# The reciprocal standard deviation of a layer norm, moved from ScalarE's square root to Newton steps on VectorE

## The chip, the cores and the metric

The kernel runs on one core of a Trainium2 chip. A core has five engines with an instruction stream each: TensorE (PE in the profile, its weight loads PEld), VectorE (DVE), ScalarE (ACT), GpSimd (POOL) and SyncE (SP, which here only issues transfers). They run beside each other and wait for each other's results through semaphores. The metric is the time of one execution on the device in microseconds (us); smaller is better.

## The reference

A graph network of two layers with residuals on 32768 nodes of 256 features, and 524288 edges sorted by target. Layer 0 is attention inside 256 blocks of 128 nodes; layer 1 sends messages along the edges in both directions and updates each node through a gate. Each layer begins with a layer norm over a node's 256 features, and relu:

```python
def _layernorm(x, axis=-1, eps=1e-5):
    m = jnp.mean(x, axis=axis, keepdims=True)
    v = jnp.var(x, axis=axis, keepdims=True)
    return (x - m) / jnp.sqrt(v + eps)

h = jnp.maximum(_layernorm(x, axis=-1), 0.0)
x = x + layer0(h, ...)        # out = softmax(Q K^T * scale + bias) V, then Wo
h = jnp.maximum(_layernorm(x, axis=-1), 0.0)
x = x + layer1(h, src, dst, edge_weight, edge_weight_n2, ...)

# layer 1: batch norm over the nodes, then
a_in  = segment_sum(feat_in[src]  * iw[:, None], dst)
a_out = segment_sum(feat_out[dst] * ow[:, None], src)
# xi = [a_in, a_out] @ W_x2i + b; gates: sigmoid, tanh; h = new + gate * (h - new)
```

What the change touches is the factor 1/sqrt(v + eps) of both layer norms: one number for each node.

## The kernel before, in words

Four parts follow each other. Up to about 960 us the edges are sorted into items, tables are made and the attention bias is gathered. Then comes the **merged stage** (1159 to 10272 us), which does two things beside each other: all of layer 0 (layer norm, attention, the second layer norm), and, edge by edge, the copying of layer-1 rows into source order. A gather stage up to 17.6 ms and a last stage of gates and output follow. The change lies in the merged stage and in the two groups of nodes that are worked off alone ahead of it (964 to 1158 us).

**The edge loop.** The edges are cut into items of 128. A round is 64 items, and each item is one step, about 2 us long. There are 68 rounds, in three phases; most are unrolled by four, and a phase's last rounds run singly. In a step (`items`, lines 1139 to 1145) the engines do, in an order written out by hand:

- `fetch` (line 1089): SP loads 128 rows of the normalised h1, 12 steps ahead;
- `spread_lanes` (1095), every fourth step: four small matmuls, 4 steps ahead;
- `select` (1099, 1100): DVE makes a one-hot matrix `oh`, 2 steps ahead, and every fourth step the selection `selT`;
- `rank` (1111): three matmuls of PE add the one-hot matrices into the running counts `R`;
- `product` (1106): PE picks each edge's row of h1;
- `place` (1123): DVE reads from `R` the place of each edge; every fourth step (1127) it adds the four together into `pi`;
- `scale` (1115, 1117): ACT multiplies the picked rows by the edge's weight, one step later;
- `scatter` (1132): POOL writes four items' rows to their places, with four indirect transfers.

The rank of a step needs the place of the step before (both touch the counts), and the place of a step needs its rank. That is the loop between PE and DVE.

**The attention work.** Each of the 64 groups holds 512 nodes, in four blocks of 128 (`GB`). One round of the edge loop carries the work of three groups at once (line 1164): `store` of group g-1, `attend` of group g, `project` of group g+1. Each function puts pieces of work at steps: `at(t)` means behind the items of step t. `project` loads x at step 5, takes mean and variance of the four blocks (`row_stats`, two at step 9 and two at 10), takes the root of all four at step 11 (line 741) and the reciprocal at 12 (785), normalises a block every third step from 13 on (768), transposes it on PE two steps later (746) and applies relu on ACT (777); then come the projections. `attend` does per block scores, maximum (861), exponential (867), transposes (873), the product with V and the output projection, and at B + 20 adds the residual and takes the second norm's mean and variance. `norm` then takes the root (741), the reciprocal (929) and `nmr`, which is minus the mean times that (930); ACT makes h1 (938), PE transposes it (746) and ACT copies it (946). Blocks 0 to 2 are done by `attend` from step 50 on, block 3 by `store` in the next round from step 1 on. `store` issues the stores of x1 (step 2), h1 (step 4) and h1's transpose (step 8) on ACT's queue, and takes the statistics of the batch norm (966, 967) at step 8.

Every engine but POOL keeps the order in which the instructions are written, step by step: first the items, then the `todo` of the step (lines 1177 to 1179):

```python
items(t, turn, 0 if t < n else n - 1, n + 64 if t < n else n)
for f in todo.get(t, ()):
    f()
```

In rounds unrolled by four, stage boundaries (line 1157) let the next iteration begin before the last has ended.

Of the kernel before, what the change touches and what calls it, by code (L numbers as in the profile page):

```python
# [11 lines left out]
F32 = mybir.dt.float32  # L12
I32 = mybir.dt.int32
AF = mybir.ActivationFunctionType
ALU = mybir.AluOpType
# [4 lines left out]
P = 128  # L20
# [5 lines left out]
GB = 4  # L26
GN = GB * P
EF = 8
EPS = 1e-5
# [331 lines left out]
def target_counts(nc, pool, cnt, off, lo, hi, name):  # L361

    a = pool.tile([P, NB], F32, name=f"{name}_a")
    nc.vector.tensor_add(a, off, cnt)
    nc.vector.tensor_scalar(a, a, float(hi), None, op0=ALU.min)
    b = pool.tile([P, NB], F32, name=name)
    nc.vector.tensor_scalar(b, off, float(lo), None, op0=ALU.max)
    nc.vector.tensor_sub(b, a, b)
    nc.vector.tensor_scalar(b, b, 0.0, None, op0=ALU.max)
    return b  # L370
# [129 lines left out]
def gnn_kernel(ctx, tc, x, src, dst, edge_attr, edge_type, w_in_e, w_out_e,  # L500
               Wq, bq, Wk, bk, Wv, bv, Wo, bo, gate_table, We, be,
               gamma, beta, W_in, b_in, W_out, b_out, W_x2i, b_x2i, W_h2h, out):
    nc = tc.nc
# [19 lines left out]
    eps = cpool.tile([P, 1], F32, name="eps")  # L523
# [57 lines left out]
    for k, (lo, hi) in enumerate(edges):  # L581
        t = target_counts(nc, cpool, dcnt, doff, lo, hi, f"dcnt{k}")
# [4 lines left out]
        at = lambda t, f: t[rs, f, 0:CS]  # L587
        of = lambda f, i: tabr_d[rs, i:i + CT, f].rearrange("c (a i) -> c a i", i=4)[:, :, 1:4]
        _, _, r = item_tables(tc, cpool, cn, f"o{k}", scnt[k], 0, T3, CS, 1, NCO[k], hi - lo, [
            ("first", of(0, 0)), ("to", of(1, LAG)),  # L590
            ("keep", at(tabb_d, 1)), ("node", at(tabb_d, 2))])
# [48 lines left out]
    with tc.tile_pool(name="ld", bufs=1) as lp:  # L640
# [7 lines left out]
        for k in range(K):  # L648
            n, node = NC1[k], itp[k][1]
# [3 lines left out]
            v = lp.tile([CI, n], F32, name="v")  # L653
# [14 lines left out]
        for k in range(K):  # L668
            left = lp.tile([P, 1], F32, name="left")
            nc.vector.tensor_scalar(left, g, -1.0, float(NG), op0=ALU.mult, op1=ALU.add)  # L670
            at = lambda i: slice(i * K + k, i * K + k + 1)
# [20 lines left out]
    with ExitStack() as c1:  # L692

        ap = c1.enter_context(tc.tile_pool(name="a_1", bufs=1))
# [15 lines left out]
        with tc.tile_pool(name="a_v", bufs=1) as vp:  # L710
            bv_c = col_vec(vp, bv, "bv_c")
            ps = a_ps.tile([P, D], F32, name="mm")
            for k in range(KC):
                t = vp.tile([P, P], F32, name=f"bv{k}")
# [8 lines left out]
        mv, rstd = ([ap.tile([P, GB] + w, F32, name=f"{n}{i}") for i in range(2)] for n, w in (("mv", [2]), ("rstd", [])))  # L723
# [13 lines left out]
            nc.vector.bn_stats(st, rows)  # L737
            nc.vector.bn_aggr(mv[i][:, b], st)

        def std(i, bs):  # L740
            nc.scalar.activation(rstd[i][:, bs], mv[i][:, bs, 1], AF.Sqrt, bias=eps)

        def transposed(name, rows):
            tp = a_ps.tile([P, KC, P], F32, name=name)
# [4 lines left out]
        def project(g, qT, kbd):  # L749

            todo, at = steps_of()

            @at(5)
            def _():
                nc.sync.dma_start(xg, x_g[g], bounds_check="skip_entire_dma")

            for b in range(GB):
                cols = slice(b * P, (b + 1) * P)
                row = {}

                @at(9 + b // 2)
                def _(b=b):
                    row_stats(0, b, xg[:, b])

                @at(13 + 3 * b)
                def _(b=b, row=row):
                    xn = row["xn"] = ab.tile([P, D], F32, name="xn")
                    nc.vector.tensor_scalar(xn, xg[:, b], mv[0][:, b, 0:1], rstd[0][:, b:b + 1],
                                            op0=ALU.subtract, op1=ALU.mult)

                @at(15 + 3 * b)
                def _(row=row):
                    row["tp"] = transposed("mx", row["xn"])

                @at(16 + 3 * b)
                def _(row=row, cols=cols):
                    nc.scalar.activation(hT[:, :, cols], row["tp"], AF.Relu)

            @at(11)
            def _():  # L780
                std(0, slice(0, GB))

            @at(12)
            def _():
                nc.vector.reciprocal(rstd[0], rstd[0])

            for m in range(KC):
                ps = {}
                mc = slice(m * P, (m + 1) * P)
                for k in range(KC):  # L790
                    @at(27 + 10 * m + k)
                    def _(m=m, k=k, ps=ps, mc=mc):
                        if k == 0:
                            ps["q"] = a_ps.tile([P, GN], F32, name="mx")
                        nc.tensor.matmul(ps["q"], wq[:, k, mc], hT[:, k], start=(k == 0), stop=(k == KC - 1))

                    @at(31 + 10 * m + k)
                    def _(m=m, k=k, ps=ps, mc=mc):
                        if k == 0:
                            ps["k"] = a_ps.tile([P, GN], F32, name="mx")  # L800
                        nc.tensor.matmul(ps["k"], wk[:, k, mc], hT[:, k], start=(k == 0), stop=(k == KC - 1))

                @at(29 + 10 * m)
                def _(m=m, ps=ps):
                    nc.scalar.activation(qT[:, m], ps["q"], AF.Identity, bias=bq_c[:, m:m + 1], scale=SCALE)

                for j in range(HC):
                    @at(33 + 10 * m + j // 2)
                    def _(m=m, j=j, ps=ps):
                        r = slice(j * DH, (j + 1) * DH)  # L810
                        to = kbd[r, m, :, j, :]
                        of = ps["k"][r].rearrange("p (b n) -> p b n", b=GB)
                        if j % 2:
                            nc.scalar.activation(to, of, AF.Identity, bias=bk_c[r, m:m + 1])
                        else:
                            nc.vector.tensor_scalar(to, of, bk_c[r, m:m + 1], None, op0=ALU.add)


            for b, t in ((0, 47), (2, 60)):
                ps = {}  # L820
                for i in range(2):
                    @at(t + i)
                    def _(b=b, i=i, ps=ps):
                        if i == 0:
                            ps["v"] = a_ps.tile([P, 2, D], F32, name="mx")
                        for k in range(KC):
                            nc.tensor.matmul(ps["v"][:, i], hT[:, k, (b + i) * P:(b + i + 1) * P], wv[:, k],
                                             start=(k == 0), stop=(k == KC - 1))

                @at(t + 2)  # L830
                def _(b=b, ps=ps):
                    nc.scalar.copy(vg[:, b:b + 2, :, 0:DH], ps["v"].rearrange("p b (h d) -> p b h d", d=DH))

            @at(63)
            def _():
                nc.gpsimd.tensor_add(xb, xg, bo_b[:, None, :].to_broadcast([P, GB, D]))

            return todo

        def attend(g, qT, kbd, bias=None):  # L840

            todo, at = steps_of()
            for b in range(GB):
                B = 1 + 14 * b
# [69 lines left out]
                def _(b=b, s=s):  # L914
                    nc.vector.tensor_add(x1g[:, b], s["y"], xb[:, b])
                    row_stats(1, b, x1g[:, b])

            norm(at, slice(0, GB - 1), B - 14 + 21)
            return todo

        def norm(at, bs, t):

            @at(t)
            def _():
                std(1, bs)

            @at(t + 1)
            def _():
                nc.vector.reciprocal(rstd[1][:, bs], rstd[1][:, bs])
                nc.vector.scalar_tensor_tensor(nmr[:, bs], mv[1][:, bs, 0], -1.0, rstd[1][:, bs],  # L930
                                               op0=ALU.mult, op1=ALU.mult)

            for n, u in enumerate(range(bs.start, bs.stop)):
                h = {}

                @at(t + 2 + 2 * n)
                def _(u=u):
                    nc.scalar.activation(h1g[:, u], x1g[:, u], AF.Relu, bias=nmr[:, u:u + 1], scale=rstd[1][:, u:u + 1])

                @at(t + 4 + 2 * n)  # L940
                def _(u=u, h=h):
                    h["tp"] = transposed("mx", h1g[:, u])

                @at(t + 5 + 2 * n)
                def _(u=u, h=h):
                    nc.scalar.copy(h1T[:, :, u * P:(u + 1) * P], h["tp"])

        def store(g):

            todo, at = steps_of()  # L950
            norm(at, slice(GB - 1, GB), 1)

            @at(2)
            def _():
                nc.scalar.dma_start(x1_g[g], x1g)

            @at(4)
            def _():
                nc.scalar.dma_start(h1_g[g], h1g)

            @at(8)
            def _():
                nc.scalar.dma_start(h1T_g[g], h1T)
                for k in range(KC):
                    st = ab.tile([P, 6], F32, name="st")
                    nc.vector.bn_stats(st, h1T[:, k])
                    nc.vector.tensor_copy(stats[:, k, ds(g, 1)], st[:, None, :])

            return todo
# [6 lines left out]
        with tc.tile_pool(name="a_k", bufs=1) as kp:  # L976
            bias = kp.tile([P, H, P], F32, name="bias0")
# [40 lines left out]
        for i in range(NM):  # L1018
            t = fp.tile([P, 4, MW], F32, name=f"msg{i}")
# [191 lines left out]
        for k in range(KC):  # L1211
            mv = ap.tile([P, 2], F32, name="bn_mv")
# [22 lines left out]
    with ExitStack() as c2:  # L1235
# [18 lines left out]
        for i in range(NR):  # L1254
            t = fp.tile([P, FW], F32, name=f"rows{i}")
# [128 lines left out]
    with ExitStack() as c3:  # L1384
# [10 lines left out]
        with tc.For_i(0, NG // UE, 1) as it:  # L1395
            for u in range(UE):
# [24 lines left out]
                for j in range(KC):  # L1421
                    gates = []
                    for n, (m, func) in enumerate(((j, AF.Sigmoid), (KC + j, AF.Tanh))):
# [7 lines left out]
                        t = gp.tile([P, GN], F32, name=f"act{n}")  # L1431
# [37 lines left out]
```

## Time and profile before

Six runs took 19746.07 to 19790.36 us, with a median of 19770.07 us. One more execution was profiled.

| | |
|---|---|
| median of six runs | 19770.07 us |
| the profiled execution | 19741.56 us |
| its span, first to last instruction | 19739.8 us |
| mean granted clock of TensorE | 0.89 |
| merged stage | 1159 to 10272 us, 68 rounds, mean 132.9 us for the 64 of ordinary length |
| square roots of line 741 in the merged stage | 62 of 128x4, 62 of 128x3, 65 of 128x1, 294 to 297 ns each |
| table loads of ACT in the merged stage, 1283 ns each | 189 for line 741, 186 for line 867, 20 for line 1115 |
| place (line 1123) | 477 ns, and 81 ns to read its sum |
| one scatter (line 1132) | 992 ns |

In the profile a row of instructions is named by its source line, engine and operation, with output and inputs by the program's names and shapes as partitions x elements. "Busy" is the time in which an engine worked; idle time is put down to what ended it. A row `DVE jk L1123 <- PE R L1111: 1100.1, 1179, 4.4` says that the DVE instruction of line 1123 waited for PE's of line 1111 for 1100.1 us in total, 1179 times, at most 4.4 us. An `ACT_TABLE_LOAD` changes the set of functions that ScalarE can evaluate; it is attributed to the instruction that it precedes. Rows of the timeline give start, duration, engine, line and operation, and in brackets the idle time ahead and what ended it.

### The profile page before, as it was taken

The numbers are of one execution on the slowest core, as the hardware profiler recorded it, in microseconds if no ns is written. First come the engines' busy times: TensorE is split into PE (matmuls) and PEld (weight loads), VectorE is DVE, ScalarE is ACT, GpSimd is POOL, SyncE is SP. The second block draws the span as 40 slices with busy tenths as digits, with TensorE's granted clock in tenths as the row PEclk, the third lists the DMA queues.
The fourth block names the chain that finished last, engine by engine and source line by source line (L and its number), as shares of the span: only waits on it lengthen the run. The fifth ranks groups of instructions, "written<-read, shape, count | busy, mean of one in ns | idle before, by whom it ended". The sixth has DMA issues, their size and how long they took to land. (4 is left out here: it accounts for less than half of the span.)

```text
span 19739.8 us, 294973 instructions
## 1 busy us (share of the span) xinstructions
PE 14927.4 (76%) x71798; PEld 10685.8 (54%) x71798; DVE 10152.4 (51%) x33904; ACT 6785.0 (34%) x17038; POOL 9335.7 (47%) x9309
## 2 busy tenths in 40 slices
PE   2077777777777777777658888787887777888889
PEld 2045555555555545555436666666666666653334
DVE  8656666656666656666444444444444444432222
ACT  0044444444444444444223333333333333320000
POOL 0034455544555444554446655555555555542222
PEclk6589998888998888989779999899999999999999
DMA  2034444444444444444437777677776777773333
GB/s 64 6 115 147 143 148 146 138 140 146 142 147 144 137 126 139 146 145 142 129 116 196 199 197 199 187 197 196 199 199 189 199 196 204 200 161 105 111 110 97
DMA packets 1839572, 2984.82 MB, mean 151 GB/s; under 512 B 300218, under 2 KB 1297687, under 8 KB 1837606
## 3 DMA queue, kind: packets, MB, share of 16 engines
q1 hardware_dynamic: 1174582, 1555.62, 27.2%
q0 software_dynamic: 430768, 1160.40, 20.6%
q10 hardware_dynamic: 232640, 251.23, 4.0%
q8 instruction: 563, 9.22, 0.2%
q14 instruction: 1019, 8.35, 0.2%
HBM read 2128.88 MB, written 1253.36 MB: 171 GB/s over the span
## 5 line engine op out<-in xcount | busy, mean ns | idle before, releaser
L1132 POOL DMA_INDIRECT msg_d<-msg,pi x4352 | 4316.0, 992 | 4547.2 <-ACT msg L1115 2164.2
L1275 POOL DMA_INDIRECT rows<-h_d,ixc x3584 | 3408.8, 951 | 2261.0 <-issue 715.0
L1123 DVE SCALAR_TENSOR_TENSOR jk<-iota,edc,R 128x256 f32<-128x256 bf16 x4352 | 2077.9, 477 | 3240.8 <-PE R L1111 1615.4
L1115 ACT ACTIVATE msg<-mp,edc 128x256 f32<-128x256 f32 x4352 | 2024.9, 477 | 4583.4 <-PE mp L1106 2975.7
L1310 ACT ACTIVATE selo<-lane_row,sl 128x128 f32<-128x128 f32 x5040 | 1663.3, 391 | 4602.7 <-DVE sl L1307 1643.3
L1289 PE MATMUL ps_i<-rows,sel 128*128 128x257 f32 x8960 | 2614.6, 412 | 782.7 <-DVE acc L1293 379.0
L1317 PE MATMUL ps_o<-m,selo 128*128 128x257 f32 x10080 | 2740.2, 411 | 569.0 <-ACT selo L1311 271.3
L1106 PE MATMUL mp<-hb,selT 128*128 128x256 f32 x8704 | 2941.3, 423 | 0.0
L1111 PE MATMUL R<-oh,ones_b 128*128 128x256 bf16 x4352 | 1282.0, 295 | 1918.2 <-DVE jk L1123 1070.6
L1317 PEld LDWEIGHTS ps_o<-m,selo 128*128 128x128 f32 x10080 | 1958.5, 204 | 967.5 <-issue 296.5
L1289 PEld LDWEIGHTS ps_i<-rows,sel 128*128 128x128 f32 x8960 | 1621.5, 205 | 1078.6 <-DVE acc L1293 430.0
L1111 PEld LDWEIGHTS <-triu 128*128 128x128 bf16 x4352 | 441.9, 102 | 2679.9 <-issue 2620.8
L1282 DVE TENSOR_SCALAR sel<-lane_row,ed 128x128 f32<-128x128 f32 x4480 | 1390.1, 359 | 937.9 <-PE idle L1290 387.1
L1106 PEld LDWEIGHTS mp<-hb,selT 128*128 128x128 f32 x8704 | 1500.7, 216 | 93.9
L1321 DVE SCALAR_TENSOR_TENSOR acc<-acc,blk,ps_o 128x257 f32<-128x257 f32 x1680 | 805.5, 479 | 1383.5 <-PE ps_o L1317 596.9
L1100 DVE TENSOR_SCALAR oh<-iota,edc 128x256 bf16<-128x256 bf16 x4358 | 1396.3, 320 | 137.2 <-PEq L1152 115.0
L1111 PE MATMUL R<-oh,tri 128*128 128x256 bf16 x4352 | 1297.2, 298 | 0.0
L1111 PE MATMUL R<-oh,triu 128*128 128x256 bf16 x4352 | 1296.5, 298 | 0.0
L1293 DVE SCALAR_TENSOR_TENSOR acc<-acc,blk,ps_i 128x257 f32<-128x257 f32 x2240 | 1070.4, 478 | 236.2 <-DMA sin_d<-acc 75.3
L1307 DVE TENSOR_SCALAR sl<-m,blk 128x3 f32<-128x3 f32 x1680 | 419.5, 250 | 1425.2 <-DMA m<-msg_d 1189.2
L1275 POOL DMA_INDIRECT rows<-h_d,ixh x896 | 851.6, 950 | 627.9 <-issue 249.4
L1311 ACT ACTIVATE selo<-selo,one 128x384 f32<-128x384 f32 x1680 | 1031.2, 614 | 55.2 <-issue 3.0
(369 smaller groups left out, 21073.1 us busy)
## 6 DMA issues: line engine op xcount, KB each, us to landing
m<-msg_d SPq DMA_DIRECT2D x1680, 396.0 KB
hb<-h_d SPq DMA_DIRECT2D x4388, 128.0 KB
sin_d<-acc SPq DMA_DIRECT2D x2240, 128.5 KB
sout_d<-acc SPq DMA_DIRECT2D x1680, 128.5 KB
msg_d<-msg,pi POOLq DMA_INDIRECT x4352
more<-sout_d ACTq DMA_DIRECT2D x128, 514.0 KB
rows<-h_d,ixc POOLq DMA_INDIRECT x3584
x_d<-x1g ACTq DMA_DIRECT2D x67, 512.0 KB
```

What stands on the lines that cost most here:

```text
L1100: nc.vector.tensor_scalar(ohs[q % NO], cn["iota1"], edc[z][:, 0, q:q + 1], None, op0=ALU.is_equal)
L1106: nc.tensor.matmul(mp, sels[q // 4 % 2][:, q % 4], hbs[q % NH], start=True, stop=True)
L1111: nc.tensor.matmul(R[:, q % 2], cn[what], ohs[of % NO], start=False, stop=False, skip_group_check=True)
L1115: nc.scalar.activation(msg[:, q % 4, 0:D], turn.pop(("mp", q)), AF.Copy, scale=edc[z][:, 1, q:q + 1])
L1123: nc.vector.scalar_tensor_tensor(jk, cn["iota1"], edc[z][:, 0, q:q + 1], R[:, q % 2], op0=ALU.is_equal, op1=ALU.mult, accum_out=turn["pf"] ...
L1132: s = nc.gpsimd.indirect_dma_start(out=msg_d[k][:], out_offset=bass.IndirectOffsetOnAxis(ap=turn["pi"][:, j:j + 1], axis=0), in_=msgs[q // ...
L1275: nc.gpsimd.indirect_dma_start(out=rows[(2 * i + r) % NR][:, 0:D], out_offset=None, in_=h1_d[:], in_offset=bass.IndirectOffsetOnAxis(ap=(i ...
L1282: nc.vector.tensor_scalar(sel[:, r], cn["lane_row"], c["ed"][:, 0, r, i:i + 1], c["ed"][:, 1, r, i:i + 1], op0=ALU.is_equal, op1=ALU.mult)
L1289: nc.tensor.matmul(ps, sel[:, r], rows[(2 * i + r) % NR], start=(r == 0), stop=(r == 1))
L1293: nc.vector.scalar_tensor_tensor(acc[0][i % NA], acc[0][(i - 1) % NA], c["blk"][:, 0, i:i + 1], c.pop(("t_ps", i)), op0=ALU.mult, op1=ALU.add)
L1310: nc.scalar.activation(sel[:, r], cn["lane_row"], AF.Abs, bias=sl[:, r:r + 1])
L1317: nc.tensor.matmul(ps, sel[:, r], m[:, r, 0:FW], start=(r == 0), stop=(r == T3 // P - 1))
```

## The change

The square root on ScalarE (`std`) and the reciprocal on VectorE are replaced by `inverse_std`, all on VectorE. It adds eps to the variance, makes a first guess of 1/sqrt from the bits of the number (a shift, and a subtraction from a constant), and improves it by three Newton steps of three instructions each. The twelve instructions depend on each other; three go to each of four consecutive steps. Tiles `v` and `u` are its own for each use.

To make room for four steps the work is placed anew. `project` runs the chain at steps 11 to 14; the normalised rows go from steps 13, 16, 19, 22 to 14, 17, 20, 22, and their transposes and relus with them. `norm` is split two and two: blocks 0 and 1 in `attend` with the chain at steps 36 to 39 and h1 from step 49 on; blocks 2 and 3 in `store` with the chain at steps 1 to 4 and h1 from step 5 on. The stores of h1 and of its transpose, with the batch norm's statistics, go from steps 4 and 8 to 8 and 12.

```diff
-        def std(i, bs):
-            nc.scalar.activation(rstd[i][:, bs], mv[i][:, bs, 1], AF.Sqrt, bias=eps)
+        def inverse_std(at, t, i, bs):
+            y = rstd[i][:, bs]
+            n = bs.stop - bs.start
+            v, u = (ap.tile([P, n], F32, name=f"is{i}{bs.start}{c}") for c in "vu")
+            @at(t)
+            def _():
+                nc.vector.tensor_scalar(v, mv[i][:, bs, 1], EPS, None, op0=ALU.add)
+                nc.vector.tensor_scalar(u.bitcast(I32), v.bitcast(I32), 1, None, op0=ALU.arith_shift_right)
+                nc.vector.tensor_scalar(y.bitcast(I32), u.bitcast(I32), -1, 0x5F3759DF, op0=ALU.mult, op1=ALU.add)
+            for j in range(3):
+                @at(t + 1 + j)
+                def _():
+                    nc.vector.tensor_mul(u, y, y)
+                    nc.vector.scalar_tensor_tensor(u, u, -0.5, v, op0=ALU.mult, op1=ALU.mult)
+                    nc.vector.scalar_tensor_tensor(y, u, 1.5, y, op0=ALU.add, op1=ALU.mult)
...
+            inverse_std(at, 11, 0, slice(0, GB))
             for b in range(GB):
+                X = (14, 17, 20, 22)[b]
-                @at(13 + 3 * b)
+                @at(X)
                 def _(b=b, row=row):
                     xn = row["xn"] = ab.tile([P, D], F32, name="xn")
-                @at(15 + 3 * b)
+                @at(X + 2)
-                @at(16 + 3 * b)
+                @at(X + 3)
-            @at(11)
-            def _():
-                std(0, slice(0, GB))
-            @at(12)
-            def _():
-                nc.vector.reciprocal(rstd[0], rstd[0])
...
-            norm(at, slice(0, GB - 1), B - 14 + 21)
+            norm(at, slice(0, GB - 2), B - 28 + 21, 13)
-        def norm(at, bs, t):
-            @at(t)
+        def norm(at, bs, t, gap):
+            inverse_std(at, t, 1, bs)
+            @at(t + 3)
             def _():
-                std(1, bs)
-            @at(t + 1)
-            def _():
-                nc.vector.reciprocal(rstd[1][:, bs], rstd[1][:, bs])
                 nc.vector.scalar_tensor_tensor(nmr[:, bs], mv[1][:, bs, 0], -1.0, rstd[1][:, bs],
...
-                @at(t + 2 + 2 * n)
+                @at(t + gap + 2 * n)
-                @at(t + 4 + 2 * n)
+                @at(t + gap + 2 + 2 * n)
-                @at(t + 5 + 2 * n)
+                @at(t + gap + 3 + 2 * n)
...
         def store(g):
-            norm(at, slice(GB - 1, GB), 1)
+            norm(at, slice(GB - 2, GB), 1, 4)
-            @at(4)
+            @at(8)
             def _():
                 nc.scalar.dma_start(h1_g[g], h1g)
-            @at(8)
+            @at(12)
             def _():
                 nc.scalar.dma_start(h1T_g[g], h1T)
```

## The prediction

> **What bounds the kernel now.** I read the page's engine rows first, then the busy time of each engine in stretches of the merged stage, then the waits of 2000 to 8000 us, then the two ScalarE lines that reload a function table, and last the order of work around one of them.
>
> ```profile
> PE 14927.4 (76%) x71798; PEld 10685.8 (54%) x71798; DVE 10152.4 (51%) x33904; ACT 6785.0 (34%) x17038; POOL 9335.7 (47%) x9309
> ```
>
> ```profile
> 2000.00:3000.00 1000.00, 787.50 (x4332) 544.14 (x4330) 624.58 (x2251) 445.56 (x1141) 499.95 (x497) 0.91 0.46 145
> 5000.00:6000.00 1000.00, 783.88 (x4321) 543.12 (x4321) 627.42 (x2265) 449.42 (x1147) 505.44 (x501) 0.91 0.46 146
> ```
>
> The columns are PE, PEld, DVE, ACT, POOL, clock, DMA share and GB/s. In the merged stage (1159 to 10272 us, 68 rounds of 64 steps) PE is busy 78%, DVE 63%, ACT 45%. No engine is full, so the order of waits decides.
>
> ```profile
> DVE jk L1123 <- PE R L1111: 1100.1, 1179, 4.4
> PE R L1111 <- DVE jk L1123: 737.3, 468, 5.7
> DVE jk L1123 <- remote: 404.7, 72, 7.6
> POOL msg_d L1132 <- ACT pr L867: 378.2, 113, 8.6
> ```
>
> PE's rank matmuls and DVE's place instruction wait for each other: a loop of two engines, step after step (us, times, longest). ScalarE is in neither of their lines; POOL's scatter (line 1132) does wait for it. Who waited for its two table lines over the whole kernel (us, times): first for line 741, the square root, then for line 867, the exponential.
>
> ```profile
>   DVE rstd L929: 44.3, 19
>   DVE rstd L785: 6.9, 12
>   PEld mx L746: 6.7, 1
> ```
>
> ```profile
>   PEld pt L873: 20.1, 43
>   PE pt L873: 6.5, 11
> ```
>
> DVE waited 51 us for the square root of line 741, of which some 10 us at each of the three phase changes, and PE 27 us for the exponential of line 867. So ScalarE's lateness is worth at most about 85 us.
>
> ```profile
> L741 ACT ACT_TABLE_LOAD x189 | 242.5, 1283 | 35.0 <-issue 31.7
> L867 ACT ACT_TABLE_LOAD x186 | 238.6, 1283 | 3.3
> L785 DVE RECIPROCAL rstd<-rstd 128x4 f32<-128x4 f32 x62 | 11.0, 177 | 20.9 <-issue 16.4 <-ACT rstd L741 4.5
> L929 DVE RECIPROCAL rstd<-rstd 128x1 f32<-128x1 f32 x65 | 10.1, 156 | 40.6 <-ACT rstd L741 40.4
> L930 DVE SCALAR_TENSOR_TENSOR nmr<-mv,rstd 128x1 f32<-128x1 f32 x65 | 10.4, 159 | 2.2
> ```
>
> And a piece of the order of time, steps 1 to 3 of one round:
>
> ```profile
> 2218.58 1.28 ACT L741 ACT_TABLE_LOAD   x1
> 2220.38 0.16 DVE L929 RECIPROCAL rstd<-rstd 128x1 f32<-128x1 f32 x1
> 2220.57 0.16 DVE L930 SCALAR_TENSOR_TENSOR nmr<-mv,rstd 128x1 f32<-128x1 f32 x1
> 2220.65 0.68 DVE L861 TENSOR_REDUCE nm<-sc 128x4 f32<-128x512 f32 x1
> 2221.25 0.28 DVE L1100 TENSOR_SCALAR oh<-iota,edc 128x256 bf16<-128x256 bf16 x1
> ```
>
> The load runs beside the loop. The reciprocal stands in DVE's line, and the place instruction of line 1123 follows the last of these rows at 2221.47 with no idle time: here DVE is the loop's bound.
>
> **What it removes.** Per round three square roots (0.30 us each) and six loads of 1.283 us: 8.6 us of ACT in a round of 133. Loads stand only before the square root and before what follows it (lines 867 and 1115), never before relu, copy or identity elsewhere, so without the square root all of them go. By the waits that frees at most 85 us over the stage, 1.3 us a round; the terms below take it where it falls. Three reciprocals go from DVE (0.5 us a round).
>
> [...]
>
> **What it adds.** Per round three chains of twelve dependent DVE instructions on 128x1 to 128x4, three in each of four steps. No row shows these exact operations on such tiles. Nearest: 156 to 177 ns busy (L785, L929, L930), 146 ns (the 64x1 copy of L1040), and at the far end 250 ns (L1307, 128x3). From the start of L929 to that of L930, which reads its result, is 0.19 us. I take 0.19, so 0.57 us a step; ends 0.45 and 0.75. A round adds 36 x 0.19 = 6.8 us of DVE, less 0.5.
>
> [...]
>
> **Where it falls.** The starts of the place instruction cut a round into steps; averaged over the 64 rounds of ordinary length (mean 132.9 us) each step has a length and the idle time of DVE and PE in it. An addition is absorbed as far as DVE is idle while PE is what the loop waits for. Per round:
>
> - Steps 1 to 4 (length 1.67, 1.64, 1.11, 1.24 us; DVE idle 0.38, 0.26, 0.22, 0.55): 0.57 more in each, less the reciprocal at 2 (0.16). If all idle time absorbs: 0.19 + 0.15 + 0.35 + 0.02 = +0.7. In part it is the wait from place to the next rank and back, which a later place only moves; if it absorbs little, +1.3. I take +0.9 (0.6 to 1.3).
> - Steps 3 to 7: the exponential is no longer behind a load; PE waited 27 us for it in all, 0.4 a round. Two transposes (0.38 us in this round) leave step 5 (PE idle 0.33 of 2.44) and come back, four of them, at 7 and 9, where PE idles 1.51 and 0.84. Together at best -1.4; if 7 and 9 are then longer by what step 5 gains, +0.5. I take -0.5, nearer the waits' row than the best case.
> - Step 8: two bn_stats (688 ns) with two copies (173 ns) leave, 1.72 us. Steps 8 and 9 last 4.83 us with DVE busy 4.44 and PE 3.01; with transposes added PE needs 3.5, so at most -1.3. I take -0.8 (-1.3 to -0.4).
> - Steps 11 to 14 (DVE idle 0.76, 0.55, 0.65, 1.32): 4 x 0.57, less a reciprocal 0.18, plus the 1.72 at step 12: 3.82 against 3.28 idle, so +0.5 at least; if each step uses only its own idle time, step 12 alone gives 0.57 + 1.72 - 0.18 - 0.55 = +1.6. I take +1.0.
> - Steps 15 to 25: normalised rows, transposes and relus shift by a step. Steps 15 to 19 end in a stall (19 lasts 4.37) that comes when two groups of four scatters (0.99 + 0.30 us each) follow on POOL without a gap. Spacing from 15 to 19 hardly changes: 0 (-0.5 to +0.5).
> - Steps 36 to 39 (DVE idle 0.27, 1.43, 0.81, 0.60): +0.30 at 36, nothing at 37 and 38, where PE is full (idle 0.11 and 0.01), and with the 0.16 of L930 +0.13 at 39. Step 37 can recover some: +0.35 (0.1 to 0.6).
> - Steps 50 to 59: a load, a reciprocal and L930 leave where DVE was idle 0.4 to 0.75, so nothing. Six transposes at 54, 56, 58 become four at 51 and 53: -0.2 (-0.7 to 0). The stall at step 55 (6.93 us) is again POOL's two groups without a gap; they stay.
> - DMAs: the stores of h1 and h1T move from steps 4 and 8 to 8 and 12, on ACT's queue, one instruction each; x1's stays. SP's fetches of h1 rows (line 1089) wait for the store of h1, SP's queue behind them (217 us in 23 waits, 13.4 at most), for rows used twelve steps later; the wait moves from step 4 to 8 with the same distance, and the load of x at step 5 now stands ahead of it: 0. The lead groups and three phase changes run serially: twelve instructions at 0.19 = 2.3 us in place of 1.28 + 0.30 + 0.16 and two handovers: 0, within 5 us in all.
>
> Sum: 0.9 - 0.5 - 0.8 + 1.0 + 0 + 0.35 - 0.2 = +0.75 us a round, x 64 = +48 us. The profiled execution took 19741.56 us (span 19739.8), so its like would take 19,790. The median of the six runs, 19770.07, lies 28 us above it, and the forecast is against that: 19,818 us. All lower ends together are -2.7 a round (-173 us), all upper ends +4.1 (+262).
>
> **Rivals.**
> - Faster: scatters start when ACT's messages are done, and POOL waited 378 us in 6000 for the exponential's line. If loads are what pushes two groups together, their end removes a 4 us stall at step 19 in half of the rounds: -130, with half of the 85 us of waits -170: 19,600. Against it: the stalls at 19 and 55 follow the place results' spacing, and single rounds without stage boundaries lack the one at 55. It decides from about 20 rounds that lose their stall.
> - No change: shifts cancel, 19,770. For it: PE is nearly full in 11 to 14 and 37 to 39, and the steps 4 to 9 have 1.7 us to give.
> - Clearly slower: nothing at 4 to 9 is recovered, because PE there waits for something else: 0.9 + 1.6 + 0.6 = +3.1 a round, 19,970. It decides if step 8 shortens by less than 0.4 us.
> - Loads remain: then 19,818 plus the 0.4 of the exponential, 19,845. The rows speak against it, since only the square root's neighbours load.
>
> **How the numbers follow.** A difference below about 0.2% (40 us) is about what a measurement of this kernel cannot tell from none. Slightly slower as summed 0.33, clearly slower 0.10, loads remain 0.02; no change 0.25; faster 0.30. Bounds of the terms do not all fall one way; from -120 to +190 us about the median leaves some 1 in 10 on each side: 19,650 to 19,960. The likeliest case's own range is 19,810 to 19,880.
>
> **What would show it.** After: no loads between 1159 and 10272 us; ACT's busy share there down from 45% to about 38%, DVE's up from 63% to 67%; steps 1 to 3 longer by 0.2 to 0.4 us each; step 8 shorter by about 0.8, step 12 longer by 1 or more; stalls at 19 and 55 as before. Wrong if steps 4 to 9 give back more than 1.3 us, if the stall at 19 goes or a new one comes, or if a small DVE instruction costs far from 0.19 us.

## The result, and the profile after

The changed kernel takes 19795.47 us, the median of 17 executions (19765.68 to 19845.12); the kernel before took 19759.2 us beside it (37 executions). The ratio is 1.0021, with a 95% interval of 1.0014 to 1.0027: slower by 36 us, a fifth of a per cent. The forecast was +48 us.

The profiled execution of the changed kernel took 19746.76 us with a span of 19745.0 us. It is the fastest of all that were taken, 49 us under the median (that of before was 18 us under its own). In it the merged stage is even 10 us shorter than before. So one pair of profiles cannot show the 36 us; it shows what moved in one execution of each. The engines' busy time in the merged stage, first of the changed kernel, then of the one before (PE, PEld, DVE, ACT, POOL, clock, DMA share, GB/s):

```profile
1159.00:10262.00 9103.00, 6966.26 (x37814) 4789.81 (x37814) 5789.74 (x22165) 3293.90 (x9316) 4521.98 (x4480) 0.89 0.45 141
```

```profile
1159.00:10272.00 9113.00, 6961.60 (x37809) 4776.49 (x37808) 5513.53 (x20090) 3852.30 (x9894) 4523.89 (x4480) 0.89 0.44 141
```

ACT lost 558 us of work: no table load is left in the stage. DVE gained 276 us, 4.3 us a round where 6.3 were forecast. PE and POOL are as before. The second row also corrects the prediction, whose 78, 63 and 45% for the merged stage are the shares between 2000 and 6000 us: over the whole stage PE was busy 76%, DVE 61% and ACT 42%; after the change DVE is busy 64% and ACT 36%. The chain's rows in the changed kernel (DVE groups by form; busy, mean ns, idle ahead):

```profile
L757 DVE SCALAR_TENSOR_TENSOR rstd<-is12u,rstd 128x2 f32<-128x2 f32 x195 | 31.4, 161 | 6.8
...
L755 DVE TENSOR_TENSOR is00u<-rstd 128x4 f32<-128x4 f32 x186 | 30.3, 163 | 0.0
...
L749 DVE TENSOR_SCALAR is12u<-is12v 128x2 int32<-128x2 int32 x65 | 12.2, 188 | 2.2
...
L748 DVE TENSOR_SCALAR is10v<-mv 128x2 f32<-128x2 f32 x62 | 21.5, 347 | 0.0
```

A small instruction takes 0.15 to 0.19 us, as the rows of before had said for their neighbours, with two exceptions: the first one of the chain in `attend` takes 0.35, and the third one of the chain in `store` (line 750) 0.28. The loop's waits between 2000 and 8000 us are almost the same as before:

```profile
DVE jk L1130 <- PE R L1118: 1022.5, 1045, 3.0
PE R L1118 <- DVE jk L1130: 747.5, 604, 6.7
...
DVE jk L1130 <- remote: 302.9, 72, 7.2
```

The last row fell by 102 us (404.7 before). What stands behind it came out only in the last experiments.

### The profile page after: what moved, and what is told of

Same layout as the page of the kernel before. It is cut to its first block, busy times and chain, and to the rows that moved or that the text cites. A ratio compares the mean times of both kernels' runs of the same rounds, so it can differ in the third digit from the quotient of the medians.

```text
span 19745.0 us, 296102 instructions
## 1 busy us (share of the span) xinstructions
PE 14910.6 (76%) x71804; PEld 10686.8 (54%) x71804; DVE 10444.9 (53%) x36060; ACT 6218.9 (31%) x16449; POOL 9329.9 (47%) x9309
```

## The experiments

The times of twelve runs come from two kinds of chip. On one, the kernel before takes 19.76 to 19.92 ms, as in the result above; on the other, 17.50 ms. Kernels are compared only by their ratio to the kernel before on the same chip, and I call the two kinds slower and quicker chips. Steps are cut as in the prediction, from one place instruction to the next. They are averaged over the same 60 rounds of every kernel, the first 62 without the two at the ends of the first two phases.

My theory was: the chain costs time on VectorE's side of the loop, the new placement gives some back, ScalarE's relief is worth little. The rivals: the placement is what costs; or the table loads are what makes the stalls.

### The moves alone, the moves without a chain, a double chain, and no root at all

The four ran on one quicker chip. The new placement, with the old root:

```diff
-            ...
+            @at(t)
+            def _():
+                nc.scalar.activation(rstd[i][:, bs], mv[i][:, bs, 1], AF.Sqrt, bias=eps)
+            @at(t + 1)
+            def _():
+                nc.vector.reciprocal(rstd[i][:, bs], rstd[i][:, bs])
```

> The new placement of the work with the old square root on ScalarE and one reciprocal on VectorE, so all table loads stay. Theory (the small VectorE instructions cost the time, the moves give some back): without the chains 1.7 us a round less than the changed kernel, so about 19,759 + 36 - 110 = 19,685 us, ratio to before 0.995 to 0.998. Rival (the moves cost it: the statistics at step 12, the transposes at 7 and 9): no faster than the changed kernel, ratio 1.002 or more.

Measured: 17419.13 us against 17503.56, ratio 0.9954 (0.9941 to 0.9968).

```diff
+        for t in rstd:
+            nc.vector.memset(t, 1.0)
...
         def inverse_std(at, t, i, bs):
-            ...
+            pass
```

> The changed kernel without its twelve instructions: the factor 1/sqrt is left out (a constant 1), neither engine computes it. Theory: 36 instructions a round fewer are 6.8 us of VectorE, of which 1.7 us were exposed, so 110 us less than the changed kernel, ratio to before 0.994 to 0.998, and a little below the kernel with the moves alone, by the loads' 0 to 85 us. Rival (the moves cost it): ratio 1.001 to 1.003, as the changed kernel.

Measured: 17312.62 us, ratio 0.9895 (0.988 to 0.991).

```diff
+        def inverse_std(at, t, i, bs):
+            one_chain(at, t, i, bs, rstd[i][:, bs], "is")
+            again = ap.tile([P, GB], F32, name=f"again{i}{bs.start}")
+            one_chain(at, t, i, bs, again[:, bs], "it")
```

> The changed kernel with each chain done twice, the second time into tiles that nobody reads, in the same steps. Theory: another 36 instructions a round of 0.19 us, 6.8 us, less of which can be absorbed than of the first: 110 to 250 us more than the changed kernel, ratio to before 1.008 to 1.015. Rival (VectorE has room, the moves cost it): within 0.2% of the changed kernel, ratio 1.000 to 1.004.

Measured: 18039.47 us, ratio 1.0312 (1.0298 to 1.0326). And the kernel before without its root:

```diff
         def std(i, bs):
-            nc.scalar.activation(rstd[i][:, bs], mv[i][:, bs, 1], AF.Sqrt, bias=eps)
+            pass
```

> The kernel before without its square root and so without table loads: the factor is a constant 1, the reciprocal of it still runs, nothing is moved. Theory (ScalarE is off the path): what waited for it, 20 to 60 us, is gained, ratio 0.997 to 0.999. Rival (the loads push POOL's scatters together and so make the stalls): 150 us or more, ratio 0.9925 or less, with fewer stalls at steps 7, 19 and 55.

Measured: 17485.91 us, ratio 0.9988 (0.9979 to 0.9997).

The last one answers the table loads: without any, in the old placement, 21 us are gained (0.0012 of 17,500). So the loads cost little on this kind of chip. The rival that they make the stalls is not tested by it: the kernel without root has no step of over 3.8 us at 19 or 55 here (41 and 59 rounds in the profile of before), and the run on a slower chip was not made. The moves are a gain here, not a cost: from "no root" to "no chain" the ratio drops by 0.0093, 163 us. So that rival falls, on this kind of chip. (The three reciprocals of a round went with them, 0.5 us of DVE, and are part of the 163.) With no chain and with two, the change of the time is larger than I expected; the next four runs gave the sizes.

### The changed kernel again, the chain unspread, and the statistics and chains moved

Again on a quicker chip. First the changed kernel as it is.

> The changed kernel once more, as it is, so that the others of this call can be compared with it on the same chip. On the chip of the first four experiments none of the stalls at steps 19 and 55 showed, and no chain to a double chain cost 727 us. Theory (a small VectorE instruction is exposed nearly whole): the single chain lies about half way between, ratio to before 1.006 to 1.011 on a chip without those stalls, and again about 1.002 on one with them. Rival (the first chain is absorbed in VectorE's idle time): 1.002 or less on either.

Measured: 17531.7 us against 17500.02, ratio 1.0016 (1.0007 to 1.0025). On the quicker chips, the change is as small a loss as on the slower ones. I had expected the single chain half way between none and two. It is not. The rival's number came, 1.002 or less, but not for its reason, that the chain is absorbed: the first chain costs 1.0016 - 0.9895 = 0.0121, 212 us; the second costs 1.0312 - 1.0016 = 0.0296, 518 us. The stage of the three kernels, without, with one and with two chains:

```profile
1146.00:9033.00 7887.00, 6465.56 (x37818) 4507.01 (x37816) 5460.40 (x19898) 3290.25 (x9316) 4509.79 (x4473) 0.95 0.51 162
```

```profile
1154.00:9263.00 8109.00, 6541.37 (x37815) 4561.72 (x37814) 5779.87 (x22166) 3290.43 (x9316) 4503.70 (x4473) 0.95 0.50 158
```

```profile
1164.00:9768.00 8604.00, 6822.59 (x37812) 4708.81 (x37812) 6067.09 (x24433) 3293.47 (x9316) 4507.97 (x4473) 0.91 0.47 149
```

The first chain adds 319 us of busy DVE and costs 212: a third is absorbed. The second adds 287 and costs 518, more than its own work. The reason stands in the columns of PE and of the clock: the same matmuls took 281 us longer, at a granted clock of 0.91 instead of 0.95. One place of the double chain, step 37 to 38 of one round:

```profile
2505.15 1.02 PE L809 MATMUL mx<-hT,wq 128*128 128x512 f32 x2
...
2507.96 0.43 PE L1087 MATMUL bc<-ident,F 64*128 64x64 f32 x4 [1.80 <-DVE selT L1110]
...
2509.65 1.91 PE L809 MATMUL mx<-hT,wq 128*128 128x512 f32 x2
```

PE waits 1.80 us for DVE, and the next pair of the same matmuls takes 1.91 us in place of 1.02; the granted clock is 0.50 from 2509 us on, and was 1.00 before. Here a late DVE is paid twice: by the wait of 1.80 us, and by a slower TensorE behind it, 0.89 us for this pair. In that kernel the rank matmuls of steps 14 and 38 run at the low clock (0.42 us each behind the slow pair above, 0.27 to 0.28 ahead of it) in 91% and 76% of the rounds; with a single chain, in 11% and in none. How long a wait must be to lower the clock, these runs do not show.

The root in the new placement, for comparison, costs 0.9954 - 0.9895 = 0.0059, 103 us, of which 0.83 us a round at step 37: the table load of the root at 36 stands ahead of exponentials of steps 36 and 37. So in the new placement the Newton chain costs about twice what the root and its loads cost.

Next, the chain in the old placement, six instructions at the root's step and six at the reciprocal's (`newton` is one step of three instructions; the first guess stands ahead of the first):

```diff
+            @at(t)
+            def _():
...
+                newton()
+            @at(t + 1)
+            def _():
+                newton()
+                newton()
```

> The kernel before with the twelve instructions in the old places, six at the step of the square root and six at the step of the reciprocal; nothing is moved, three blocks and one as before. Theory (exposed nearly whole, and the moves help): slower than the changed kernel, which has the moves' 80 to 90 us: ratio to before 1.008 to 1.016. Rival (spreading and moving cost it): faster than the changed kernel.

Measured: 17637.32 us, ratio 1.0077 (1.0063 to 1.0091); just under the range that was expected. Against the kernel without root (0.9988) the chain costs 0.0089 here, 156 us. It is not the spreading that makes the changed kernel better than this one; in its four steps the chain costs 212 us. It is the other moves. By step, against the kernel without root: 1 and 2 are longer by 1.73 us a round, 50 and 51 by 1.02, while 9 and 14 are 1.35 shorter. In step 9 the kernel without root is longer than 3.8 us in 27 rounds and this one in none, though nothing was moved; why, the runs do not show.

Then the batch norm's statistics, later:

```diff
-            @at(12)
-            def _():
-                nc.scalar.dma_start(h1T_g[g], h1T)
-                for k in range(KC):
+            for k in range(KC):
+                @at(27 + k)
+                def _(k=k):
                     st = ab.tile([P, 6], F32, name="st")
                     nc.vector.bn_stats(st, h1T[:, k])
```

The transfer stays at 12.

> The changed kernel with the two statistics instructions (and their copies) of the batch norm at steps 27 and 28 in place of 12; TensorE is busy there all the time and VectorE idle for 1.4 us of each. Theory: step 12 gets 1.1 us shorter, steps 27 and 28 stay, 70 us less than the changed kernel, 0.35% of before. Rival (the wait moves on to steps 13 to 15): less than 25 us.

Measured: 17385.8 us, ratio 0.9931 (0.9918 to 0.9945), 146 us less than the changed kernel: twice what I expected. Step 12 of one round, changed kernel:

```profile
2371.50 0.48 DVE L1130 SCALAR_TENSOR_TENSOR jk<-iota,edc,R 128x256 f32<-128x256 bf16 x1
...
2371.90 0.69 DVE L973 BATCH_NORM_STATS2 st<-h1T 128x6 f32<-128x512 f32 x1
...
2372.25 0.27 PE L1118 MATMUL R<-oh,tri 128*128 128x256 bf16 x1
...
2372.62 0.17 DVE L974 COPY stats<-st 128x6 f32 x1
2372.70 0.69 DVE L973 BATCH_NORM_STATS2 st<-h1T 128x6 f32<-128x512 f32 x1
2373.43 0.17 DVE L974 COPY stats<-st 128x6 f32 x1
2373.51 0.15 DVE L755 TENSOR_TENSOR is00u<-rstd 128x4 f32<-128x4 f32 x1
2373.70 0.16 DVE L756 SCALAR_TENSOR_TENSOR is00u<-is00u,is00v 128x4 f32<-128x4 f32 x1
2373.89 0.16 DVE L757 SCALAR_TENSOR_TENSOR rstd<-is00u,rstd 128x4 f32<-128x4 f32 x1
2373.97 0.28 DVE L1107 TENSOR_SCALAR oh<-iota,edc 128x256 bf16<-128x256 bf16 x1
2374.17 0.48 DVE L1130 SCALAR_TENSOR_TENSOR jk<-iota,edc,R 128x256 f32<-128x256 bf16 x1
```

With the statistics late:

```profile
2348.34 0.47 DVE L1133 SCALAR_TENSOR_TENSOR jk<-iota,edc,R 128x256 f32<-128x256 bf16 x1
...
2348.74 0.16 DVE L755 TENSOR_TENSOR is00u<-rstd 128x4 f32<-128x4 f32 x1
...
2348.94 0.16 DVE L756 SCALAR_TENSOR_TENSOR is00u<-is00u,is00v 128x4 f32<-128x4 f32 x1
...
2349.13 0.16 DVE L757 SCALAR_TENSOR_TENSOR rstd<-is00u,rstd 128x4 f32<-128x4 f32 x1
...
2349.41 0.48 DVE L1133 SCALAR_TENSOR_TENSOR jk<-iota,edc,R 128x256 f32<-128x256 bf16 x1
```

In the first, the rank is done at 2372.52 and DVE takes until 2374.17 to reach the next place. In the second, the step has 1.07 us, the length that steps 3 and 8 have in the kernel without a chain (1.06). By this comparison, which is with other steps, a part of a chain is free here. The statistics at 27 and 28, beside a busy PE, are free as well (both steps the same to 0.01 us). Besides the 1.58 us at step 12, steps 51 to 53 became 1.02 us shorter together; why those, I did not find out.

Last, the chains of the second norm where DVE is idle beside a busy PE:

```diff
-            norm(at, slice(0, GB - 2), B - 28 + 21, 13)
+            norm(at, slice(0, GB - 2), (37, 38, 41, 42), 49)
-            norm(at, slice(GB - 2, GB), 1, 4)
+            norm(at, slice(GB - 2, GB), (4, 5, 6, 7), 8)
```

The stores of h1 and of its transpose go to steps 11 and 15.

> The one before it, and the chains where VectorE is idle beside a busy TensorE: blocks 0 and 1 at steps 37, 38, 41, 42 in place of 36 to 39, blocks 2 and 3 at 4 to 7 in place of 1 to 4 (h1 from step 8, its stores at 11 and 15). Theory: steps 1 to 3 and 36 get their 1.0 to 1.3 us back, steps 4 to 7 lose some 0.5: 30 to 60 us less than with the late statistics alone, ratio to before 0.995 to 1.001. Rival (an instruction of the chain costs the same anywhere): no difference.

Measured: 17333.98 us, ratio 0.99 (0.9885 to 0.9916), 52 us less than the one before it. The difference is as expected, the ratio is below the expected 0.995 to 1.001. Steps 1 to 3 gave back 1.0 us a round and 36 0.36, and steps 5 to 7 took 0.65 and 37 0.44; 38, 41 and 42 have a part of the chain and the same length as without (to 0.01 us). This version beats both kernels on a quicker chip, by a whole per cent.

### The same ideas on a slower chip

These three were to show that the root, well placed, is the better choice. They ran on a slower chip, where the kernel before took 19924.24 us. The first has the root with the placement of the change and the late statistics (the edits of the moves alone and of the late statistics together).

> The new placement with ScalarE's square root and VectorE's one reciprocal, all table loads kept, and the statistics of the batch norm at steps 27 and 28. Theory (the chain is what the change costs, the placement what it gains): 146 us less than the moves alone, ratio to before 0.986 to 0.989, and some 100 us less than the same with the Newton chains. Rival (with the statistics out of step 12 the chain has room and costs nothing): no faster than that one, 0.993.

Measured: 20077.93 us, ratio 1.0079 (1.0061 to 1.0097). The second is the kernel before with the late statistics alone.

> The kernel before with nothing changed but the statistics of the batch norm, from step 8 to 27 and 28. Theory: steps 8 and 9 lose the 2.1 us that they lost with the moves, times 64 is 135 us, ratio to before 0.992. Rival (the gain of the moves at steps 8 and 9 came from the transposes): within 0.3% of before.

Measured: 19960.65 us, ratio 1.0015 (1.0005 to 1.0024). The third (stores of h1 and of its transpose at steps 11 and 15):

```diff
-            norm(at, slice(0, GB - 2), B - 28 + 21, 13)
+            norm(at, slice(0, GB - 2), (40, 41), 49)
-            norm(at, slice(GB - 2, GB), 1, 4)
+            norm(at, slice(GB - 2, GB), (5, 6), 8)
```

> As the first of this call, and the square roots where no exponential follows within three steps: blocks 0 and 1 at step 40 in place of 36 (whose load stood ahead of the exponentials of steps 36 and 37), blocks 2 and 3 at 5 in place of 1. Theory: step 37 loses 0.8 us, steps 2 and 6 together 0.3: some 70 us less than the first, ratio 0.982 to 0.986, faster than before and than every version with the chain. Rival (ScalarE is off the path wherever the root stands): within 20 us of the first.

Measured: 19986.67 us, ratio 1.0035 (1.0022 to 1.0047): 91 us less than the first, and slower than before. The 91 us are about the size that was expected of the root's place, but not there: step 37 is only 0.17 us shorter a round, while 11 and 7 are shorter by 0.75 and 0.54 and 55 is longer by 0.74.

All three expectations of the ratio failed. The second's rival has its number (within 0.3% of before), and the first's too, on a chip for which it was not meant. Nor do the moves show a gain here: with the statistics late in both, the new placement with the root is 0.0064 slower than the old one, and 0.0020 with the root in its better place. The late statistics, worth 146 us in the changed kernel on a quicker chip, are worth nothing in the kernel before on this one. These are two kernels on two chips, and no run separates the kernel from the chip. A stretch of the kernel before, on a slower chip, shows what is different (place, the last matmul of the rank, and the scatters on POOL):

```profile
4224.17 0.48 DVE L1123 SCALAR_TENSOR_TENSOR jk<-iota,edc,R 128x256 f32<-128x256 bf16 x1 [0.38 <-PE R L1111]
...
4225.86 0.27 PE L1111 MATMUL R<-oh,tri 128*128 128x256 bf16 x1
...
4226.27 0.99 POOL L1132 DMA_INDIRECT msg_d<-msg,pi  x1 [0.30 <-issue]
...
4227.56 0.99 POOL L1132 DMA_INDIRECT msg_d<-msg,pi  x1 [0.30 <-issue]
...
4228.85 0.99 POOL L1132 DMA_INDIRECT msg_d<-msg,pi  x1 [0.30 <-issue]
...
4230.15 0.99 POOL L1132 DMA_INDIRECT msg_d<-msg,pi  x1 [0.30 <-issue]
...
4232.52 0.48 DVE L1123 SCALAR_TENSOR_TENSOR jk<-iota,edc,R 128x256 f32<-128x256 bf16 x1 [7.47 <-remote]
```

The rank ends at 4226.13, as far as the profile's modelled ends of matmuls tell. DVE has been idle since 4225, and the place starts at 4232.52, 6.4 us later. The trace lists TensorE's semaphore as the only one that it waits for, and has an update of that semaphore at 4232.49. The waits of 2000 to 8000 us name such a wait "remote". On the quicker chips (the kernel without root, and the changed one) no such row is among the sixty largest. The kernel before with the late statistics, on the slower chip, has:

```profile
DVE jk L1126 <- remote: 553.7, 112, 7.9
```

It was 404.7 us in the profile of before, 149 us less. By step, against that profile, step 8 is 0.97 us shorter, as intended; steps 5, 11, 15 and 27 are 1.48, 0.99, 1.09 and 0.80 longer, and 19 is 1.65 shorter. Steps of over 3.8 us rose from 181 to 256 (at step 5 from 2 to 42 rounds). But the profile of before was not taken with these runs, in which the same kernel took 165 us more than in the result; how much of the shift is the chip's, this pair does not tell. What it shows is that the long steps do not go when DVE is relieved: this kernel has them, at partly other steps.

To see whether the chain costs the same on a slower chip, I ran the kernel without it once more.

> The changed kernel without its twelve instructions once more (the factor is left out, a constant 1), for a chip of the slower kind, where the kernel before takes 19.7 to 19.9 ms and TensorE's signals come late; on the quicker kind (17.5 ms) the chain cost 219 us. Theory (late signals, not VectorE, set the time of the stage there, so that relief of VectorE is given back): ratio to before 0.998 to 1.006, no more than 60 us below the changed kernel. Rival (the chain is exposed there as on the quicker kind): ratio 0.989 to 0.992.

It fell on a quicker chip again: 17324.48 us against 17507.17, ratio 0.9892 (0.9876 to 0.9909). That repeats the 0.9895 on another chip, and leaves the question open.

## Why the prediction was right, and where it was not

The sign, the size and the range hold: +48 us forecast, +36 measured on the slower chips; on the quicker ones 0.16%. The quicker chips also give the account in three parts, in ratios to before: the root's end -0.0012 (-21 us), the moves with the end of the reciprocals -0.0093 (-163 us), the chain +0.0121 (+212 us), together +0.0016. Two large terms cancel. The forecast had the same two with these signs, both too small, so that the number came so close is in part luck. More so on the slower chips, where the result was taken: there the parts were not measured alone, and the time from a finished rank to a place that DVE is free for, beyond the 39 ns that it usually takes, adds up to 1229 us of the merged stage in the profile of before and 963 in the changed kernel's. That is a term of which the forecast had nothing, and the difference of the two, 266 us, is over five times the forecast.

Two of the prediction's own signs of being wrong came. Steps 4 to 9 gave back 2.0 us on the quicker chip (1.2 in the pair of profiles on the slower ones), where 1.3 was the limit; and in that pair the stall at 19 went, in 31 of 41 rounds. By its steps, us a round:

| part | forecast | quicker chip, before without root to changed | slower chip, before to changed (one profile each) |
|---|---|---|---|
| steps 1 to 4 | +0.9 | +1.08 | +0.71 |
| steps 5 to 7 (forecast for 3 to 7) | -0.5 | -0.13 | -1.33 |
| steps 8 to 10 | -0.8 | -2.19 | +0.31 |
| steps 11 to 14 | +1.0 | +0.80 | +0.98 |
| steps 15 to 25 | 0 | -0.14 | -1.39 |
| steps 26 to 35 | 0 | 0.00 | +0.46 |
| steps 36 to 39 | +0.35 | +0.72 | +0.82 |
| steps 40 to 49 | 0 | -0.01 | -0.11 |
| steps 50 to 56 | -0.2 | +0.54 | -0.53 |
| steps 57 to 63 and 0 | 0 | -0.07 | -0.10 |
| sum | +0.75 | +0.60 | -0.19 |

- **The root's end.** Right. All loads of the stage went; the waits had bounded what they held up at 85 us, and it is 21 on the quicker chip. The rival "loads remain" is out. What the loads cost on a slower chip was not measured.
- **The price of an instruction.** Right: 0.15 to 0.19 us but for the two exceptions, 0.19 from start to start.
- **Steps 1 to 4 and 11 to 14.** Right within their bounds, on both kinds of chip. That idle DVE time absorbs beside a busy PE held at 38, 41 and 42, and by the comparison above at 12 without the statistics; at 1 to 3, where PE idles too, the chain costs 1.19 of 1.7. It did not hold at 37, as the next item shows.
- **Steps 36 to 39.** Too low, and over the upper end of 0.6. I let 37 absorb its part, because PE has no idle time there. On the quicker chip the chain costs 0.39 us there: PE's idle time in 37 rose from 0.04 to 0.74 us, as its matmuls then wait for DVE.
- **Step 8.** Mis-sized: -0.8, with -1.3 as the lowest, was -2.1 on the quicker chip (step 8 -1.2, step 9 -0.9). The 0.9 are the long ninth steps of the kernel without root; the chain in the old places ended them as well, so it is not shown that the moves did. The kernel before was not profiled on a quicker chip; if it does not have them there, the root's end is worth up to 57 us more than the 21 and the moves that much less than 163. In the pair of profiles on the slower chips step 8 lost 0.6, but step 9 gained 0.7.
- **The stalls at 19 and 55.** That they stay was wrong for 19. In the profiled execution the rounds with a step 19 of over 3.8 us fell from 41 to 10, and those with such a step 55 from 59 to 54. But 7 went from 12 to 23, 9 from none to 13, 27 from 2 to 10. The rival that reckoned on the end of the stall at 19 had the event (31 rounds, where 20 were to decide) and not the gain.
- **What I did not see.** That the trace of before shows a chip whose signals come late (6.4 us in the stretch above). I took the burst of waits for a property of the kernel's order; on the quicker chips the same order has none at those steps.

What stays open: the chain's, the moves' and the loads' cost apart on a slower chip, since the runs without the chain, with the moves alone and without the root all fell on quicker ones; what the late signals come from; and whether the version that is 1% faster on quicker chips is faster on slower ones.

## What to carry to other kernels

In this loop of two engines, on the quicker chips, work put on DVE was free in steps where PE was what the loop waited for (38, 41 and 42, the same to 0.01 us), but not in all of those (0.39 us at 37), and at 1 to 3, where both had idle time, most of it was paid (1.19 of 1.7 us). In another loop, look for that step by step, not in the busy share of the engine. A change that moves several things is a sum of terms of both signs: on the quicker chips the moves were worth 163 us and the new arithmetic cost 212, so the part that made the headline was the part to leave out there. And before a small gain is believed, run it on more than one chip: the new placement with the old root gained 0.5% on a quicker chip, and with the statistics later still it was 0.8% slower than before on a slower one.

## What the runs showed of the hardware that I had not expected

- **Chips of two kinds.** The same kernel took 17.50 ms on some and 19.76 to 19.92 ms on others. Between 11.5 and 14.5 ms, in the gather stage, DMA moved 196 GB/s in the kernel before on a slower chip and 234 GB/s in the changed one on a quicker one.
- **Late signals.** From the end of the rank's last matmul to the place, where DVE was idle, there were 38 to 41 ns in each of 1731 cases of the changed kernel on a quicker chip (2000 to 8000 us), beside running scatters too. In the kernel before on a slower chip the median is 39 ns as well, but the mean 0.40 us over 1727 cases and the longest 6.6 us. They gather where eight scatters follow on POOL with less than 0.4 us between them: 91% of 78 such runs in the kernel before held a wait of the place of over 3.5 us, against 6% of 864 runs of four. On a quicker chip the same instruction has the same 0.99 us, runs of eight and twelve occur, and none of the 1731 places starts over 41 ns after its rank.
- **The clock as a multiplier.** The second chain cost 1.8 times its own busy time (518 us for 287); PE, made to wait, came back at a lower clock, 0.91 in place of 0.95 over the stage.
